# Gate and up values of layer 1 by seven block products in place of eight

## The chip, the cores and the metric

The kernel runs on one core of one Trainium2 chip. The metric is the device time of one execution in microseconds (us): the median of three runs before the change is 770.57 us (769.84 to 771.42). The core has a matrix engine (TensorE, PE in the profile; its weight loads are PEld), a vector engine (VectorE, DVE), an activation engine (ScalarE, ACT), a general engine (GpSimd, POOL) and a queue for transfers (SyncE, SP). All data are float32 but the small flags of the sparsifying, which are bfloat16.

## The reference

Two layers work on `x` of shape 4 x 512 x 256. Each is a layer norm, an attention part and an MLP part on the same normed rows, added to `x`. Layer 0 is an mLSTM with an MLP, and a mixture of low-rank experts. The change touches layer 1 alone:

```python
xn = _layernorm(x, axis=-1)
x = x + _L1_attn_ref(xn, L1_attn_weight_qkv, L1_attn_weight_out) \
      + _L1_ffn_ref(xn, L1_ffn_w_gate, L1_ffn_w_up, L1_ffn_w_down)

# attention: l is the batch of 4, n the 512 positions: each position attends over the 4 rows
attn = jnp.einsum('lnhd,mnhd->nhlm', q, k)            # 16 heads of 16
causal = jnp.tril(jnp.ones((l, l), dtype=bool))
attn = jax.nn.softmax(jnp.where(causal, attn, -jnp.inf), axis=-1)
out = jnp.einsum('nhlm,mnhd->lnhd', attn, v).reshape(l, n, e)
return jnp.einsum('lne,fe->lnf', out, weight_out)

# MLP: 256 -> 1024 -> 256; of each four neighbours of h the two largest stay
h = jax.nn.silu(x @ w_gate) * (x @ w_up)
return _sparsify_2to4(h) @ w_down
```

The attention is causal over the four rows of the batch, so the first row attends to itself alone, with weight one, whatever its q.

## The kernel before

A *block* is 128 positions of all four batch rows, 512 columns once transposed; there are four blocks. Partitions hold features or positions, 128 at a time.

Layer 1's rows are normed (`layernorm`), transposed on PE into `xnT` (2 tiles of 128 features x 512 columns; `front_rows`), and then used by three streams. `rows(j)` goes over the 1024 inner features in tiles of 128, in two groups of four: for each tile two matrix products (`project`, one for each 128 of the 256 input features) make `gp` from the gate weights and ACT takes its Silu; two more make `up`, and DVE multiplies them into `hs`. The weights' columns are laid out so that the four tiles of a group hold the four neighbours of the 2:4 rule, which `sparsified` then applies with DVE comparisons on `hm`, the absolute values. `attention_rows(j)` makes q, k and v for each of the four batch rows and `attend_rows` the scores, with products on POOL (`pd`) and sums on DVE (`sc`, `st`, `o`). `finish_rows(j)` sums attention (`oT` with `aoT`) and MLP (`hs` with `f_down`) in PSUM (`yp`), adds them to `x` on DVE and stores.

The order is made when the program is built. The streams are Python generators; `Flow` asks each when it could go on, by a clock of estimated ends (`Clock`), and takes the next that is ready; ties go by `turn`. `flow.wait` yields the time at which named tiles, and so many of the eight PSUM banks, will be there; `flow.soon` asks again a little later. What comes out is one fixed order for each engine (`keep_in_program_order`), which each engine follows strictly. At run time only semaphores are waited for, so an instruction that waits holds all behind it on its engine.

SBUF is reused across layers by tag: layer 1's gate weights lie where layer 0's `wguT` was, its up weights in `lora`, its q, k, v weights in `WdT`, its down weights in `w_gate`. The profile names tiles by these tags: `gp<-xnT,wguT` is layer 1's gate, `up<-xnT,lora` its up, `yp<-w_gate,hs` its down. All recorded instructions carry the line of one helper (L221), so groups are told apart by their tiles.

Of the kernel before, what the change touches and what calls it, by code (L numbers as in the profile page):

```python
# [9 lines left out]
AF = mybir.ActivationFunctionType  # L10
# [17 lines left out]
FAR = 3.0e4  # L28
BANKS = 8
AHEAD = 4  # L30


@with_exitstack
def layers_kernel(ctx: ExitStack, tc: tile.TileContext, io: dict, out: bass.AP):
# [193 lines left out]
    class Flow:  # L228
# [29 lines left out]
        def spare(self):  # L258

            return max(clock.free["dve"], self.now + 0.2)  # L260

        def wait(self, *aps, banks=0, over=False):

            while True:
                t = clock.ready(*aps, reads=over)
                room = clock.room(banks) if banks else 0.0
                if room > 1e8:
                    room = self.soon()
                yield max(t, room)
                if not banks or clock.room(banks) <= self.now:  # L270
                    return
# [201 lines left out]
    def project(ps, w, xT, lo, n):  # L473

        for k in range(KD):
            mm(ps[0:n, :], w[:, k, lo : lo + n], xT[:, k, :], start=(k == 0), stop=(k == KD - 1))

# [902 lines left out]


    qkvT = weight("qkvT", 3 * D, "WdT", NFC * D)
    f_gate = weight("f_gate", FF, "wguT", 4 * DFF)
    f_up = weight("f_up", FF, "lora", 2 * DFF + NFC * E * R)
    f_down = weight("f_down", D, "w_gate")
    aoT = weight("aoT", D, "w_out")


    with ExitStack() as l1:
# [3 lines left out]

        def attend_rows(j, q, k, v):

            sc = new(sm, [P, B, B, AH], "sc", 2)
            pool.memset(sc, LOWEST)
            for l in range(B):  # L1400
                m = l + 1
                pd = new(wk1, [P, B, D], "pd", 2)
                pool.tensor_tensor(
                    out=pd[:, 0:m, :], in0=k[:, 0:m, :],
                    in1=q[:, l : l + 1, :].to_broadcast([P, m, D]), op=ALU.mult)
                yield from flow.wait(pd)
                dve.tensor_reduce(
                    sc[:, l, 0:m, :], pd[:, 0:m, :].rearrange("p m (h d) -> p m h d", d=ADH),
                    AX.X, ALU.add)
            st = new(sm, [P, B, AH], "st", 2)  # L1410
            by_m = sc.rearrange("p l m h -> p l h m")
            dve.tensor_reduce(st, by_m, AX.X, ALU.max)
            stb = st.unsqueeze(2).to_broadcast([P, B, B, AH])
            dve.tensor_tensor(sc, sc, stb, ALU.subtract)
            act.activation(sc, sc, AF.Exp)
            yield from flow.wait(sc)
            dve.tensor_reduce(st, by_m, AX.X, ALU.add)
            dve.reciprocal(st, st)
            dve.tensor_tensor(sc, sc, stb, ALU.mult)
            o = new(wk1, [P, B, D], "o", 1)  # L1420
            for l in range(B):
                m = l + 1
                pd = new(wk1, [P, B, D], "pd", 2)
                pool.tensor_tensor(
                    out=pd[:, 0:m, :].rearrange("p m (h d) -> p (m h) d", d=ADH),
                    in0=v[:, 0:m, :].rearrange("p m (h d) -> p (m h) d", d=ADH),
                    in1=sc[:, l, 0:m, :].rearrange("p m h -> p (m h)").unsqueeze(2).to_broadcast(
                        [P, m * AH, ADH]),
                    op=ALU.mult)
                yield from flow.wait(pd)  # L1430
                dve.tensor_reduce(
                    o[:, l, :], pd[:, 0:m, :].rearrange("p m c -> p c m"), AX.X, ALU.add)
            while j >= 2 and j - 2 not in out_of:
                yield flow.soon()
            oT = new(wk1, [P, KD, S], "oT", 2)
            for k in range(KD):
                yield from flow.wait(o, banks=1)
                transposed(lambda l, k: o[:, l, k * P : (k + 1) * P], oT, k)
            outs[j] = oT

        def sparsified(j, hs):


            BF = mybir.dt.bfloat16

            def flags(n, tag, bufs=2):
                return new(wk1, [P, n, S], tag, bufs, BF)

            hm = new(wk1, [P, 4, S], "hm", 2)
            for n in range(0, 4, 2):  # L1450
                yield from flow.wait(hs[:, n : n + 2, :])
                act.activation(hm[:, n : n + 2, :], hs[:, n : n + 2, :], AF.Abs)
            yield from flow.wait(hm)

            c0123 = flags(2, "c0123")
            dve.tensor_tensor(c0123, hm[:, 0:4:2, :], hm[:, 1:4:2, :], ALU.is_ge)
            yield flow.soon()
            c0213 = flags(2, "c0213")
            dve.tensor_tensor(c0213, hm[:, 0:2, :], hm[:, 2:4, :], ALU.is_ge)
            yield flow.soon()  # L1460
            rest = flags(2, "rest", 1)
            c12, d30 = rest[:, 0, :], rest[:, 1, :]
            dve.tensor_tensor(c12, hm[:, 1, :], hm[:, 2, :], ALU.is_ge)
            dve.tensor_tensor(d30, hm[:, 3, :], hm[:, 0, :], ALU.is_gt)
            yield flow.soon()

            t03, t21 = flags(2, "t03", 1), flags(2, "t21", 1)
            dve.tensor_tensor(t03, c0123, c0213, ALU.add)
            dve.tensor_tensor(
                t21, c0213, rest[:, 0:1, :].to_broadcast([P, 2, S]), ALU.add)  # L1470
            yield flow.soon()
            keep = new(wk1, [P, 4, S], "keep", 2, BF)
            for n, (t, other, op) in enumerate((
                    (t03[:, 0, :], d30, ALU.is_gt), (t21[:, 1, :], c0123[:, 0, :], ALU.is_gt),
                    (t21[:, 0, :], c0123[:, 1, :], ALU.is_le), (t03[:, 1, :], d30, ALU.is_le))):
                dve.tensor_tensor(keep[:, n, :], t, other, op)
            yield flow.soon()
            for n in range(0, 4, 2):
                dve.tensor_tensor(
                    hs[:, n : n + 2, :], keep[:, n : n + 2, :], hs[:, n : n + 2, :], ALU.mult)  # L1480
                yield flow.soon()
            halves.setdefault(j, []).append(hs)

        def finish_rows(j):
# [40 lines left out]
        def attention_rows(j):  # L1525
            while j not in xTs:
                yield flow.soon()
            xT = xTs[j]
            q, k, v = (new(wk1, [P, B, D], n, 1) for n in "qkv")
            for l in range(B):  # L1530
                for name, lo, n in (("qk_ps", 0, 2 * D), ("v_ps", 2 * D, D)):
                    yield from flow.wait(xT, banks=1)
                    ps = mm_ps(name)
                    for kk in range(KD):
                        mm(ps[:, 0:n], xT[:, kk, l * P : (l + 1) * P], qkvT[:, kk, lo : lo + n],
                           start=(kk == 0), stop=(kk == KD - 1))
                    if lo == 0:
                        act.mul(q[:, l, :], ps[:, 0:D], ADH**-0.5)
                        act.copy(k[:, l, :], ps[:, D : 2 * D])
                    else:  # L1540
                        act.copy(v[:, l, :], ps[:, 0:D])
            yield from attend_rows(j, q, k, v)

        def attention_of_all_rows():
            for j in range(NJ):
                yield from attention_rows(j)

        def rows(j):
            xT = xTs[j]
            if j + 1 < NJ:  # L1550
                flow.add(front_rows(j + 1), 10)
            for f0 in range(0, NF, 4):
                hs = new(wk1, [P, 4, S], "hs", 4)
                gated.setdefault(j, []).append(hs)
                for n in range(4):
                    yield from flow.wait(banks=1)
                    gp = mm_ps("gp")
                    project(gp, f_gate, xT, (f0 + n) * P, P)
                    act.activation(hs[:, n, :], gp, AF.Silu)
                    yield from flow.wait(banks=1)  # L1560
                    up = mm_ps("up")
                    project(up, f_up, xT, (f0 + n) * P, P)
                    dve.tensor_tensor(hs[:, n, :], up, hs[:, n, :], ALU.mult)
                flow.add(sparsified(j, hs))
            flow.add(finish_rows(j), turn=1)

        def all_rows():
            for j in range(NJ):
                flow.until(lambda: j in xTs)
                yield from rows(j)  # L1570
            written.add(NJ - 1)

        flow.add(attention_of_all_rows())
        flow.run(all_rows())
        flow.until(lambda: not flow.streams)


# [38 lines left out]
```

## Time and profile before

| | us |
|---|---|
| median of three runs | 770.57 (769.84 to 771.42) |
| the profiled execution's own time | 770.89 |
| its span, first to last instruction | 769.1 |
| around the span | 1.8 |
| layer 1, from the first `qk_ps` on PE to the end | 230.1 |
| PE busy / weight loads | 762.4 / 518.2 |
| DVE / ACT / POOL busy | 466.9 / 225.1 / 162.8 |

A row of a group gives the operation, the tiles (out from in), the shapes and the count, then busy time, the mean of one in ns, and the idle time of its engine just before, with what ended it. PE's rows include the time in which a product runs through the pipeline, beside the next one; the chain of work shows the spacing. The clock that was granted to PE was 1.0 in all slices.

### The profile page before, as it was taken

How to read it: one execution, taken by the hardware profiler on the slowest of the kernel's cores; microseconds unless marked ns; L12 is line 12 of the kernel's file. 1: busy time of each engine (PE TensorE's matmuls, PEld its weight loads, DVE VectorE, ACT ScalarE, POOL GpSimd, SP SyncE). 2: the span in 40 equal slices, each digit the busy share in tenths (PEclk: the TensorE clock that was granted, in tenths of full speed). 3: DMA queues.
4: the chain of work that ended last, by engine and by line, in shares of the span. 5: the costliest groups of instructions: out<-in, count | busy, mean ns of one | idle time of the engine just before them, and what ended most of it. 6: DMA issues, size and time to landing. Idle time of an engine off the chain costs nothing.

```text
span 769.1 us, 9739 instructions
## 1 busy us (share of the span) xinstructions
PE 762.4 (99%) x3792; PEld 518.2 (67%) x3792; DVE 466.9 (61%) x1075; ACT 225.1 (29%) x457; POOL 162.8 (21%) x154
## 2 busy tenths in 40 slices
PE   9999999999999999999999999999999999999998
PEld 6786777766667875865777774747545664664487
DVE  6787576956544987633377635341376965934971
ACT  4334224332313343212133312010444224214300
POOL 6221051232041320240030041000333224013100
PEclk9999999999999999999999999999999999999999
DMA  7930000300000200000031110001000000000001
GB/s 236 291 109 1 2 1 0 97 15 0 2 1 1 111 0 1 2 1 0 1 111 36 75 43 13 1 0 55 0 1 0 1 27 1 0 29 0 1 14 42
DMA packets 18959, 25.44 MB, mean 33 GB/s; under 512 B 2784, under 2 KB 12768, under 8 KB 18912
## 3 DMA queue, kind: packets, MB, share of 16 engines
q1 hardware_dynamic: 17824, 24.53, 9.9%
q8 instruction: 30, 0.49, 0.3%
q10 hardware_dynamic: 1088, 0.28, 0.2%
q14 instruction: 17, 0.14, 0.1%
HBM read 22.65 MB, written 2.16 MB: 32 GB/s over the span
## 4 chain that ended last, share of the span: by engine, by line
PE 91%; DVE 8%; issue 1%; DMA 0%; POOL 0%; ACT 0%; SPq 0%; DVEq 0%; POOLq 0%
PE yp L221 18%; PE chunk L221 16%; PE up L221 14%; PE gp L221 14%; PE acc L221 10%; PE qk_ps L221 4%; PE pt L221 2%; PE vp L221 2%; PE o_ps L221 2%; PE v_ps L221 2%; PE lp L221 2%; DVE sl L221 1%; PE qk L221 1%; PE hv L221 1%; DVE tmp L221 1%; PE q_ps L221 1%
## 5 line engine op out<-in xcount | busy, mean ns | idle before, releaser
L221 PE MATMUL chunk<-low,lora 128*128 128x256 f32 (+1 forms) x384 | 86.3, 384 | 1.3 <-DVE he_pair L221 1.1
L221 ACT ACTIVATE sl<-chunk 128x256 f32<-128x256 f32 x132 | 50.7, 384 | 113.7 <-PE chunk L221 100.9
L221 PE MATMUL chunk<-xnT,wguT 128*128 128x256 f32 (+1 forms) x384 | 83.8, 383 | 0.0
L221 PEld LDWEIGHTS chunk<-xnT,wguT 128*128 128x128 f32 (+1 forms) x384 | 63.7, 181 | 20.5 <-issue 8.9
L221 PEld LDWEIGHTS chunk<-low,lora 128*128 128x128 f32 (+1 forms) x384 | 63.5, 181 | 17.1 <-issue 4.4
L221 DVE SCALAR_TENSOR_TENSOR sl<-sl,chunk 128x256 f32<-128x256 f32 x132 | 54.6, 414 | 23.9 <-ACT sl L221 23.5
L221 PE MATMUL up<-featT,w_up 128*128 128x512 f32 x128 | 60.4, 594 | 0.0
L221 PE MATMUL gp<-featT,w_gate 128*128 128x512 f32 x128 | 60.3, 593 | 0.0
L221 PE MATMUL up<-xnT,lora 128*128 128x512 f32 x128 | 60.2, 592 | 0.0
L221 PE MATMUL gp<-xnT,wguT 128*128 128x512 f32 x128 | 60.2, 592 | 0.0
L221 PE MATMUL yp<-w_down,hid 128*128 128x256 f32 x256 | 56.4, 379 | 0.0
L221 PE MATMUL yp<-w_gate,hs 128*128 128x256 f32 x256 | 56.1, 379 | 0.0
L221 PEld LDWEIGHTS yp<-w_down,hid 128*128 128x128 f32 x256 | 48.5, 190 | 8.2 <-issue 1.9
L221 PEld LDWEIGHTS yp<-w_gate,hs 128*128 128x128 f32 x256 | 48.6, 190 | 6.6
L221 DVE SCALAR_TENSOR_TENSOR tmp<-tmp,gp 128x512 f32<-128x512 f32 x32 | 22.0, 687 | 45.6 <-ACT tmp L221 45.6
L221 ACT ACTIVATE tmp<-gp 128x512 f32<-128x512 f32 x32 | 19.1, 597 | 95.0 <-PE gp L221 95.0
L221 POOL TENSOR_TENSOR pd<-k,q 128x256 f32<-128x256 f32 (+3 forms) x16 | 24.6, 1539 | 97.8 <-ACT k L221 96.5
L221 PEld LDWEIGHTS gp<-xnT,wguT 128*128 128x128 f32 x128 | 24.2, 190 | 28.8 <-issue 28.0
L221 PEld LDWEIGHTS up<-xnT,lora 128*128 128x128 f32 x128 | 24.2, 190 | 28.4 <-issue 27.5
L221 PEld LDWEIGHTS gp<-featT,w_gate 128*128 128x128 f32 x128 | 24.2, 190 | 28.1 <-issue 27.7
L221 PEld LDWEIGHTS up<-featT,w_up 128*128 128x128 f32 x128 | 23.9, 190 | 27.2 <-issue 26.1
L221 PE MATMUL acc<-tmp,lora 128*128 128x512 f32 x80 | 40.8, 598 | 0.0
(221 smaller groups left out, 1188.3 us busy)
## 6 DMA issues: line engine op xcount, KB each, us to landing
ct<-m_dram SPq DMA_DIRECT2D x8, 1024.0 KB, 8.5
x<-in_x SPq DMA_DIRECT2D x3, 512.0 KB, 9.7
out<-x SPq DMA_DIRECT2D x6, 256.0 KB, 2.2
w_gate<-in_w_gate SPq DMA_DIRECT2D x1, 1024.0 KB, 7.0
w_up<-in_w_up SPq DMA_DIRECT2D x1, 1024.0 KB, 7.6
w_down<-in_w_down SPq DMA_DIRECT2D x1, 1024.0 KB, 10.2
wguT<-in_f_gate SPq DMA_DIRECT2D x1, 1024.0 KB, 5.0
lora<-in_f_up SPq DMA_DIRECT2D x1, 1024.0 KB, 4.9
```

What stands on the lines that cost most here:

```text
L221: return tc.keep_in_program_order(f(*args, **kw))
```

## The change

Gate and up values of a group of four inner tiles are made from blocks. The weights of two tiles are taken as a 2 x 2 matrix of blocks (`a11` ... `a22`: input half by tile parity), the transposed rows as another (`b11` ... `b22`: input half by column half, 256 columns each). Strassen's scheme, in Winograd's form, replaces eight block products by seven and needs sums of blocks: `sides` makes those of the weights once, on POOL, into room that layer 0 has left; `other_sides` makes those of the rows (`xd`) for each block, on DVE for the first and on POOL for the others. The sums after the products are made in PSUM: `Sevens.pairs` adds products into banks `x`, `y` and `z`, and takes copies of what stands in them at a point, on ACT (into `z`, and into SBUF rooms cut from `w_up` and `w_down`), which DVE adds later. The four quarters of a result reach `gate` or `up` through `took`: Silu on ACT; the multiply on DVE for the first column half and on POOL for the second. One identity product writes bank `z` at the start.

Besides, the first batch row's q and its scores are left out, and its attention output is a copy of v; the layer's streams get other waits and turns (`unhurried`, `turn`, the start of `attend_rows` as a stream of its own), and `all_rows` becomes one of them.

```diff
+        def unhurried(self):
+            while True:
+                yield max(clock.free["dve"] - LITTLE, self.now + 0.1)
+                if clock.free["dve"] <= self.now + LITTLE:
+                    return
...
+    def sides(w, rooms, by):
+        v = w.rearrange("p k (q m c) -> p k q m c", m=2, c=P)
+        for i in range(len(rooms) // 3):
+            q = slice(2 * i, 2 * i + 2)
+            a11, a12, a21, a22 = v[:, 0, q, 0, :], v[:, 1, q, 0, :], v[:, 0, q, 1, :], v[:, 1, q, 1, :]
+            s1, s2, s4 = rooms[3 * i : 3 * i + 3]
+            for o, a, b, op in ((s1, a21, a22, ALU.add), (s2, s1, a11, ALU.subtract),
+                                (a21, a11, a21, ALU.subtract), (s4, a12, s2, ALU.subtract)):
+                by.tensor_tensor(out=o, in0=a, in1=b, op=op)
...
+    def other_sides(xT, t, by):
+        b11, b12, b21, b22 = (xT[:, k, h * HALF : (h + 1) * HALF] for k in range(2) for h in range(2))
+        for n, a, b in ((0, b12, b11), (1, b22, t[:, 0, :]), (2, b22, b12), (3, b21, t[:, 1, :])):
+            by.tensor_tensor(out=t[:, n, :], in0=a, in1=b, op=ALU.subtract)
...
+            def product(ps, m, n, start=False, stop=False):
+                for i in range(2):
+                    mm(ps[:, i * HALF : (i + 1) * HALF], a[m](q0 + i), b[n],
+                       start=start and i == 0, stop=stop and i == 1, skip_group_check=True)
...
+            def added(ps, t, m, half):
...
+                    yield from flow.wait(ps, t)
+                    dve.tensor_tensor(t, ps, t, ALU.add)
...
+                    took(m, half, t, lambda: None)
+                flow.add(rest(), turn=-2)
...
+            def first():
+                yield from flow.wait(*b.values(), banks=2)
+                x, y = (mm_ps(n) for n in "xy")
...
+                product(x, "a11", "b11", start=True)
+                while self.users:
+                    yield flow.soon(0.2)
+                self.users += 1
+                act.copy(z, x)
+                yield 0
+                product(y, "s1", "t1", start=True)
+                t2 = copied(y)
+                yield from read(x)
+                product(x, "s2", "t2")
+                t3 = copied(x)
+                yield clock.ready(z)
+                product(z, "a12", "b21", stop=True)
+                took(0, 0, z, free_z)
+                yield from read(y)
+                product(y, "s4", "b22", stop=True)
+                added(y, t3, 0, 1)
+                kept.extend((x, t2))
+            def last():
+                x, t = kept
+                yield from read(x)
+                product(x, "s3", "t3")
+                added(x, t, 1, 1)
+                yield from read(x)
+                product(x, "a22", "t4", stop=True)
+                took(1, 0, x, lambda: clock.held.discard(x.tensor.name))
...
+    gate_sides, up_sides = (sides(w, rooms[i : i + 6], pool) for w, i in ((f_gate, 0), (f_up, 6)))
...
-            for l in range(B):
+            for l in range(1, B):
...
+            act.copy(o[:, 0, :], v[:, 0, :])
...
-                for name, lo, n in (("qk_ps", 0, 2 * D), ("v_ps", 2 * D, D)):
+                for name, lo, n in (("qk_ps", 0 if l else D, 2 * D if l else D), ("v_ps", 2 * D, D)):
...
+        sevens = Sevens(room)
+        mm(sevens.z, ident, xTs[0][:, 0, :], start=True, stop=True)
...
+        def following_rows(j):
+            yield from front_rows(j)
+            bs[j] = other_sides(xTs[j], room_of_sides(), pool)
...
-                for n in range(4):
-                    yield from flow.wait(banks=1)
-                    gp = mm_ps("gp")
-                    project(gp, f_gate, xT, (f0 + n) * P, P)
-                    act.activation(hs[:, n, :], gp, AF.Silu)
-                    yield from flow.wait(banks=1)
-                    up = mm_ps("up")
-                    project(up, f_up, xT, (f0 + n) * P, P)
-                    dve.tensor_tensor(hs[:, n, :], up, hs[:, n, :], ALU.mult)
-                flow.add(sparsified(j, hs))
...
+                        u = t.rearrange("p (i n) -> p i n", i=2)
+                        if half:
+                            pool.tensor_tensor(out=h, in0=u, in1=h, op=ALU.mult)
+                        else:
+                            dve.tensor_tensor(h, u, h, ALU.mult)
...
+                for a, took in ((gate_sides, gate), (up_sides, up)):
+                    first, last = sevens.pairs(a, b, f0 // 2, took)
+                    yield from first
+                    flow.add(last)
+                flow.add(then(), turn=-1)
             flow.add(finish_rows(j), turn=1)
...
-        flow.add(attention_of_all_rows())
-        flow.run(all_rows())
+        flow.add(all_rows())
+        flow.add(attention_of_all_rows())
         flow.until(lambda: not flow.streams)
```

## The prediction

> **What bounds the kernel now.** I read the busy shares first, then layer 1 alone as one stretch, then the chain that ended last, then groups by shape, and for single hand-offs the timeline. The names are those of the diff: a call of `pairs` makes products P1 to P7 in its order (P1 `a11·b11`, P2 `s1·t1`, P3 `s2·t2`, P4 `a12·b21`, P5 `s4·b22`, P6 `s3·t3`, P7 `a22·t4`). A, B, C, D before a number are a block's four calls in order: gate and up of the first four tiles, gate and up of the last four.
>
> Busy shares, then the stretch from 539 us (layer 1's first `qk_ps`) to the end; its columns are the stretch's length, then PE, PEld, DVE, ACT, POOL busy us with counts, and the granted clock:
> ```profile
> PE 762.4 (99%) x3792; PEld 518.2 (67%) x3792; DVE 466.9 (61%) x1075; ACT 225.1 (29%) x457; POOL 162.8 (21%) x154
> ...
> 539.00:769.10 230.10, 226.90 (x762) 139.49 (x760) 145.61 (x230) 71.01 (x123) 50.70 (x38) 1.00 0.03 10
> ```
> TensorE (PE) is the bound in every part, at full clock, and in layer 1 it is idle only at the very end. So what a change takes off PE shows in the time, if no wait replaces it.
>
> The chain in order of time (start, us, what), two places in layer 1:
> ```profile
> 559.96 1.72 PE gp L221 x4
> 561.67 1.72 PE up L221 x4
> ...
> 731.45 34.55 PE yp L221 x160
> 766.00 0.02 issue
> 766.02 0.42 DVE x L221
> ```
> Four 512-wide instructions take 1.72 us, 0.4295 each; 160 of 256 columns take 34.55 us, 0.2159 each. A float32 product is two instructions.
>
> Groups by shape (busy, mean ns of one | idle before):
> ```profile
> L221 PE MATMUL gp<-xnT,wguT 128*128 128x512 f32 x128 | 60.2, 592 | 0.0
> L221 PE MATMUL yp<-w_gate,hs 128*128 128x256 f32 x256 | 56.1, 379 | 0.0
> L221 PEld LDWEIGHTS yp<-w_gate,hs 128*128 128x128 f32 x256 | 48.6, 190 | 6.6
> L221 ACT COPY oT<-pt 128x512 f32<-128x512 f32 x8 | 4.3, 591 | 0.1
> L221 DVE TENSOR_TENSOR hs<-up,hs 128x512 f32<-128x512 f32 x32 | 21.9, 684 | 28.2 <-PE up L221 22.2 <-ACT hs L221 4.8 <-ACT hm L221 1.2
> L221 POOL TENSOR_TENSOR pd<-k,q 128x512 f32<-128x512 f32 x4 | 5.1, 1268 | 7.2 <-ACT k L221 7.2
> ```
> The means of PE (592, 379) hold 0.163 us of pipeline beyond the issue spacing; only the spacing adds up. The weight load of 190 ns lies under each 216 ns instruction.
>
> **The change, part by part.**
>
> *Products.* Before, gate and up of layer 1 are 256 instructions of 512 columns: 256 x 0.4295 = 110.0 us. After, there are 16 calls (4 blocks of rows, 2 groups of four tiles, gate and up) of 7 products of 2 x 2 instructions of 256 columns: 448 x 0.2159 = 96.7 us. PE: -13.2. Unlike gate's, a weight load now comes per 256 columns, as in `yp`, whose spacing I used.
>
> *q of the first row.* One `qk_ps` per block goes from 512 to 256 columns: 4 x 0.86 = -3.4 us of PE. Its ACT, POOL and DVE work goes too: ACT 4 x 0.384, replaced by a copy `o<-v` of 0.37; POOL 4 x (0.73 + 0.62); DVE 4 x (0.42 + 0.41) and a quarter of the score operations, some 5.3 us.
>
> *`z`.* One identity product of 512 columns: +0.86.
>
> PE in sum: -13.2 - 3.4 + 0.9 = **-15.8 us**.
>
> *Weight sides on POOL.* 16 operations of 128x256, 0.73 each by `pd<-k,q 128x256`: 11.7 us. POOL's order puts them behind the `rstd` at 491.2 and the next POOL work of before starts at 541.9. `f_up` was issued at 432.6 and landed 4.9 us later. So they run from 492 to 504 beside layer 0's MLP, and block 0's transposed rows are not needed before 539: nothing. Were that room gone, 11.7 us would stand before P2. No DMA moves: SP's order is the same, and so is every engine's up to layer 1 but for these.
>
> *Sides of the rows* (`xd`): block 0 has four DVE operations (0.42 each) after layer 0's last `x<-yp`, done some 2.6 us into layer 1; P1 starts after 11.2 us of `z`, `qk_ps`, `v_ps` and transposes. The other blocks' 12 operations are POOL's (8.7 us), one block ahead: nothing.
>
> *Copies and adds.* ACT gets three 128x512 copies a call, 48 x 0.59 = 28.3 us; DVE two adds from PSUM, 32 x 0.684 = 21.9, and gives half of the up multiplies (16 x 0.684 = 10.9) to POOL, where they cost 16 x 1.27 = 20.3. Two table loads fewer (9 to 7). Layer 1 in sum, against some 214 us: DVE 145.6 + 21.9 - 10.9 + 1.7 - 5.3 = 153 (71%); ACT 71 + 28.3 - 2.6 = 97; POOL 50.7 + 20.3 + 8.7 - 5.4 = 74. None becomes the bound by its sum.
>
> *New waits on PE.* P3 writes `x` again, so it waits for ACT's copy of P1; P7 waits for DVE's add that reads P6; a call's P1 copy into `z` waits for the last call's reader of `z`. A PE wait holds all products behind it. Where P1, P2, P3 follow each other: P1 issues to 0.864, is readable at 1.03, ACT is done at 1.03 + 0.03 + 0.59 = 1.65, P3 is due at 1.73: no wait, margin 0.08 less the hand-back. ACT never writes PSUM in this trace; its copies from PSUM to SBUF (0.59) are the nearest row, and a 128x1024 one (1.05, `hm`) an upper bound: 0.4 x 16 = +6 us. I take 0.59, the same size and engine. P7: in the built order at least 2.6 us of other products stand between P6 and P7 (C6 to C7 in the last block: D3, D4, D5), against 0.16 + 0.68 + 0.1 = 0.95 for the add, if DVE is free.
>
> DVE is densest in block 1, where the first block's second sparsifying, the next block's layernorm and block 1's attention meet. Walked with these durations from a free DVE, it has no gap for some 15 us; the reader of `z` ends 0.8 us later than the bank is written, which costs `x` of the next P3 0.1 us, and the transposes wait 0.45 us for `xn`. That is 0.6 us in the worst block. There POOL matters:
> ```profile
> 568.89 1.21 DVE L221 TENSOR_TENSOR c<-hm 128x1024 bf16<-128x1024 f32 x1
> 572.16 1.71 DVE L221 TENSOR_TENSOR c<-hm 128x1024 bf16<-128x1024 f32 x1
> ...
> 570.85 1.94 POOL L221 TENSOR_TENSOR pd<-v,sc 128x1024 f32<-128x1024 f32 x1 [3.00 <-DVE o L221]
> ```
> The same comparison takes 1.21 us alone and 1.71 when it starts under a POOL operation, ending 1.1 us after that one's end. 28 more such operations (29 us) could lengthen DVE by nothing to 29 us. [...] Even 153 + 29 = 182 us leaves DVE under PE, so it costs only where PE waits for DVE. Zero waits is the low end; one hold of 1.27 us for each of the 16 P7 less its slack of 1.6 us is still nothing, but queued behind a sparsifying step of 2.4 us it is 2 us a call in blocks 1 and 2, up to +8. I take **+1.5 us**, near the walk.
>
> *The end.* After the last P7, 24.2 us of `yp` (row block 2: 13.8; block 3's attention and first half: 10.4) cover the last sparsifying, which waits on DVE behind `x2<-yp` until 13.8 and then needs some 7.5 us: 21.4. It holds by 2.8 us, so the end stays `yp`, `x`, store, as before.
>
> Sum on the profiled execution: 770.9 - 15.8 + 1.5 = 756.6; the median of the runs is 0.3 below the profiled one: **756.3 us**.
>
> **Rivals.**
>
> (R1) *Hand-offs eat half.* ACT's write to PSUM is slow (+6) or DVE's adds come late in blocks 1 and 2 (+8): about 764. For it: DVE's 71% and the POOL hold above; against it: the slack in the order.
>
> (R2) *Every return waits; slower.* Place: P3 and P7, the two products that write a bank just read. If nothing stood in between, each would cost a read (0.16 + 0.68 + 0.1 = 0.95): 32 x 0.95 = 30, so 785. It decides from 1.0 us of waiting a call (15.8 / 16). Against it: layer 0's `chunk` accumulates in the same way, with ACT and DVE reading between the steps, and in its longest run in the chain 56 of them take 11.64 us, 0.208 each.
>
> (R3) *Weight loads show; slower.* 192 more weight loads of 0.19 us on PE would be +36.5: 791. The `yp` spacing (0.216 with a 0.190 load each) speaks against it: a load that could not overlap would give 0.406. [...]
>
> **How the numbers follow.** Mine 0.72 (its own range 754.5 to 759), R1 0.18, R2 0.05, R3 0.03, and 0.02 for a gain eaten to within the noise. No waits at all gives 754.8; take 0.7 off for rates: low 754. The high end takes in R1: 766. What this kernel's runs can tell from no change is about 0.2%, 1.5 us. Faster: 0.72 + 0.18 = 0.90; within: 0.02; slower: 0.08.
>
> **What would show it.** Right: `qk_ps` starts at 539 as before; `x`, `y`, `z` products sum to 448 instructions at 0.216 us; PE idle in layer 1 under 3 us; ACT's `z<-x` near 0.59; the chain still PE; the last DVE `hs` ends before its `yp`. Wrong: PE idle before `x` released by DVE `w_up` or `w_down` or by ACT (R1 or R2), products above 0.22 us (R3), or a PE wait before the last 16 `yp`.

## The result and the profile after

The median of four runs is **763.99 us** (763.43 to 766.31), against 770.97 (769.84 to 771.42) before on the same chip: a ratio of 0.9918 [0.9906, 0.993]. The change makes the kernel 7.0 us faster by the medians (6.3 by the ratio), where 14.3 were forecast. The direction and the range (754 to 766) hold; the likeliest time, 756.3 with its own range to 759, does not. The time of rival R1 (764) came out, mostly by another way than R1's, as shown below.

The profiled execution of after is the slowest of its four, 766.31 us with a span of 764.6, so it shows a little more loss than the median has. Its busy shares, and the chain's shares by engine, from the page:

```profile
PE 752.8 (98%) x3986; PEld 557.4 (73%) x3986; DVE 493.3 (65%) x1087; ACT 247.4 (32%) x503; POOL 206.3 (27%) x190
...
PE 81%; DVE 17%; issue 1%; ACT 1%; POOL 0%; DMA 0%; DVEq 0%; POOLq 0%
```

Layer 1 as one stretch (length; PE, PEld, DVE, ACT, POOL busy us with counts; granted clock; DMA share; GB/s):

```profile
540.00:770.00 230.00, 216.59 (x955) 177.80 (x953) 169.65 (x242) 93.59 (x169) 83.57 (x59) 0.98 0.03 10
```

DVE has 17% of the chain, where before had 8. The span ends at 764.6, so PE is idle for 8.0 us of 224.6 in layer 1, against 3.2 of 230.0, all at the end, before. DVE is busy there for 169.65 us, where the sum gave 153, and the granted clock is 0.98 instead of 1.00.

Three places of the chain in order of time (start, us, what): the first block's products, the place that lost most, and the end.

```profile
551.45 0.86 PE x L222 x4
552.31 0.86 PE y L222 x4
...
599.80 0.60 DVE w_down L222
600.40 4.15 DVE xn L222 x3
604.55 0.04 issue
604.59 1.65 PE pt L222 x6
606.24 1.71 PE z L222 x4
...
730.37 31.09 PE yp L222 x144
```

A product of four instructions takes 0.86 us, as forecast, and the end is the unbroken run of `yp` that was forecast. But at 600.40 the chain leaves PE: three `xn` take 4.15 us on DVE, and the product behind them takes 1.71 us, twice its 0.86.

What lay under these `xn`, from the timelines of DVE, POOL and PE (start, us, engine and line, operation, out from in; in brackets the idle time before and what ended it):

```profile
600.32 4.54 DVE L222 TENSOR_SCALAR xn<-x,mv,rstd 128x256 f32<-128x256 f32 x4
...
599.68 1.50 POOL L222 TENSOR_TENSOR pd<-v,sc 128x768 f32<-128x768 f32 x1
601.13 1.32 POOL L222 TENSOR_TENSOR hs<-w_down,hs 128x512 f32<-128x512 f32 x1
602.41 1.98 POOL L222 TENSOR_TENSOR pd<-v,sc 128x1024 f32<-128x1024 f32 x1
...
602.65 0.33 PE L222 MATMUL pt<-ident,xn 128*128 128x128 f32 x1 [0.89 <-DVE xn L222]
604.59 1.65 PE L222 MATMUL pt<-ident,xn 128*128 128x128 f32 x6 [1.61 <-DVE xn L222]
```

Three POOL operations follow each other without a gap; the four `xn` start under the first and end just after the last. PE stands before the transposes twice, and all products behind them wait with it.

A smaller wait, at 593, is at a hand-off for which the prediction had slack, P6 to P7 of block 1's first gate call (PE's timeline):

```profile
591.16 1.03 PE L222 MATMUL x<-xd,wguT 128*128 128x256 f32 x4
592.02 1.03 PE L222 MATMUL x<-xd,lora 128*128 128x256 f32 x4
594.00 1.10 PE L222 MATMUL x<-xd,wguT 128*128 128x256 f32 x4 [0.95 <-DVE w_up L222]
```

The first row is P6 and the last P7; between them stands one other product, 0.86 us.

The granted clock about that place (columns as in the stretch above):

```profile
600.00:605.00 5.00, 2.50 (x11) 1.34 (x10) 5.00 (x6) 1.63 (x3) 4.39 (x3) 0.89 0.00 0
605.00:611.00 6.00, 6.00 (x19) 4.99 (x19) 6.00 (x6) 1.77 (x3) 5.32 (x5) 0.52 0.00 0
611.00:620.00 9.00, 9.00 (x46) 7.82 (x45) 6.96 (x14) 4.61 (x10) 0.78 (x2) 1.00 0.00 1
```

PE is busy for half of the first five microseconds. Then it has work without a break, but six microseconds at 0.52 of its clock; after that the full clock is back.

To sum up what PE lost, take the distance from the start of each PE instruction of layer 1 to the start of the next, less the issue spacing of its size (0.4295, 0.2159 and 0.1088 us for 512, 256 and 128 columns). What is left is called *slip* below. After has 10.6 us of it: 7.5 of waits (2.9 before the `xn` transposes at 601 to 605, 1.4 before a P7 at 593, 1.25 before transposes at 636, 1.2 before those of `o` at 653, the rest small) and 3.1 of half clock behind the first of these. The forecast had +1.5 for it. A further 0.8 us of the profiled execution lies ahead of layer 1, whose first product starts at 540.00 instead of 539.17; in the profiled executions of the other kernels below it starts between 538.4 and 540.3. So 9.1 more slip and 0.8 of late start make 9.9, against the 9.7 by which the profiled execution missed its sum (766.3 against 756.6).

The groups of DVE and POOL that hold the difference (busy, mean ns of one | idle before):

```profile
L222 DVE TENSOR_TENSOR c<-hm 128x1024 bf16<-128x1024 f32 x16 | 23.3, 1480 | 4.6 <-ACT hm L222 4.6
L222 DVE TENSOR_TENSOR hs<-keep,hs 128x1024 f32<-128x1024 bf16 x16 | 22.1, 1402 | 0.0
...
L222 DVE TENSOR_SCALAR xn<-x,mv,rstd 128x256 f32<-128x256 f32 x12 | 11.9, 1049 | 1.1 <-POOL rstd L222 1.1
L222 DVE TENSOR_TENSOR w_up<-x,w_up 128x512 f32<-128x512 f32 x16 | 11.0, 685 | 9.5 <-PE x L222 9.5
...
L222 POOL TENSOR_TENSOR hs<-w_down,hs 128x512 f32<-128x512 f32 x8 | 15.2, 1894 | 52.6 <-DVE w_down L222 52.6
```

The first three of them in before:

```profile
L221 DVE TENSOR_TENSOR c<-hm 128x1024 bf16<-128x1024 f32 x16 | 20.9, 1318 | 0.0
L221 DVE TENSOR_TENSOR hs<-keep,hs 128x1024 f32<-128x1024 bf16 x16 | 19.3, 1214 | 0.0
...
L221 DVE TENSOR_SCALAR xn<-x,mv,rstd 128x256 f32<-128x256 f32 x12 | 6.1, 567 | 1.1 <-POOL rstd L221 1.1
```

Their means were 1318, 1214 and 567 ns. The adds from PSUM (`w_up<-x`) stay at their 685. POOL's multiply was priced at 1268 and takes 1894 in these eight, 1534 in the eight from `w_up`. That it is held as well is inferred from this; no run isolates it.

### The profile page after: what moved, and what is told of

Same layout as the page of the kernel before. It is cut to its first block, busy times and chain, and to the rows that moved or that the text cites. A ratio compares the mean times of both kernels' runs of the same rounds, so it can differ in the third digit from the quotient of the medians.

```text
span 764.6 us, 10254 instructions
## 1 busy us (share of the span) xinstructions
PE 752.8 (98%) x3986; PEld 557.4 (73%) x3986; DVE 493.3 (65%) x1087; ACT 247.4 (32%) x503; POOL 206.3 (27%) x190
## 4 chain that ended last, share of the span: by engine, by line
PE 81%; DVE 17%; issue 1%; ACT 1%; POOL 0%; DMA 0%; DVEq 0%; POOLq 0%
PE yp L222 16%; PE chunk L222 14%; PE acc L222 9%; PE up L222 7%; PE gp L222 7%; PE x L222 6%; PE y L222 3%; PE qk_ps L222 2%; PE pt L222 2%; DVE xn L222 2%; DVE sl L222 2%; PE vp L222 2%; PE o_ps L222 2%; PE lp L222 2%; PE z L222 2%; DVE tmp L222 2%
## 5 line engine op out<-in xcount | busy, mean ns | idle before, releaser
L222 POOL TENSOR_TENSOR ss<-ss,mhalf 128x32 f32<-128x32 f32 x4 | 22.1, 5526 | 73.1 <-DVE ss L222 73.1
L222 PE MATMUL acc<-WdT,hid 128*128 128x256 f32 (+1 forms) x192 | 40.6, 384 | 0.0
L222 PEld LDWEIGHTS acc<-WdT,hid 128*128 128x128 f32 (+1 forms) x192 | 32.9, 189 | 6.6 <-issue 2.3
L222 POOL TENSOR_TENSOR rstd<-rstd,mhalf 128x4 f32<-128x4 f32 (+1 forms) x11 | 9.6, 872 | 101.4 <-DVE rstd L222 68.7
L222 DVE TENSOR_TENSOR tmp<-chunk,sl 128x256 f32<-128x256 f32 x80 | 33.9, 424 | 2.8
```

The lines of the kernel that those rows point to most:

```text
L222: return tc.keep_in_program_order(f(*args, **kw))
```

## The experiments

The theory after the result: POOL's operations that read SBUF hold up DVE's operations there (T1, *holds*), DVE is then late for PE, and where PE stands as it does at 601 to 605 (2.5 us of 3.1) the half clock comes on top. Its rivals: the sums of work or the order alone make DVE late, whatever POOL reads (T2, *order*); or the new products themselves, or the rest of the change, cost more than priced (T3). Each kernel ran four times or more, beside the kernel before on the same chip; diffs are against after where nothing else is said. A re-planned kernel is one whose planner found another order.

### Which part of the change misses its price

**The new streams without first-row q, eight products.** Gate and up are made as before, so products, sides, copies and adds of the scheme fall away; the rest of the change stays.

```diff
-        sevens = Sevens(room)
-        mm(sevens.z, ident, xTs[0][:, 0, :], start=True, stop=True)
...
+                for n in range(4):
+                    yield from flow.wait(banks=1)
+                    gp = mm_ps("gp")
+                    project(gp, f_gate, xTs[j], (f0 + n) * P, P)
+                    act.activation(hs[:, n, :], gp, AF.Silu)
+                    yield from flow.wait(banks=1)
+                    up = mm_ps("up")
+                    project(up, f_up, xTs[j], (f0 + n) * P, P)
+                    dve.tensor_tensor(hs[:, n, :], up, hs[:, n, :], ALU.mult)
...
-                for a, took in ((gate_sides, gate), (up_sides, up)):
-                    first, last = sevens.pairs(a, b, f0 // 2, took)
```

> The changed kernel's new streams, turns and waits and its missing first q, but gate and up from eight products as before, no sides, no z. PE has 3.4 us less than before. If the streams cost nothing by themselves: 767 to 768.5. If the new order brings waits of its own: 769 to 772.

Measured: 766.61 (766.49 to 768.11), ratio 0.9948 [0.9931, 0.9965] to a before of 771.28, with 0.1 us of slip and not one wait of PE in layer 1. That is a little faster than both expected ranges. So 4.7 us come from the streams and the left-out q (priced at 3.4, inside the interval of 2.7 to 5.3); in the profiled executions layer 1 is 3.6 us shorter than in before. The seven products bring only the 2.6 us from here to 763.99, where 12.3 (13.2 less 0.86) were priced. The miss is in what the products bring with them.

**Before, with only the first row's q left out.**

```diff
-            for l in range(B):
+            for l in range(1, B):
...
+            act.copy(o[:, 0, :], v[:, 0, :])
...
-                for name, lo, n in (("qk_ps", 0, 2 * D), ("v_ps", 2 * D, D)):
+                for name, lo, n in (("qk_ps", 0 if l else D, 2 * D if l else D), ("v_ps", 2 * D, D)):
```

(against before)

> The kernel before with the first row's q and scores left out and nothing else of the change. By the price of the prediction PE loses 4 x 0.86 = 3.4 us and nothing comes in its place: 767.5, 0.9955 of before. A rival, that the shorter attention moves a wait, gives 768.5 to 771.

Measured: 769.65 (768.65 to 769.87, ten runs), ratio 0.9981 [0.9972, 0.999]: 1.4 us, not 3.4. PE's waits in layer 1 (total us, times, longest) say why:

```profile
PE pt L221 <- DVE o L221: 1.1, 1, 1.1
```

Before had no such wait. With less PE work before them, the transposes of `o` at 574 us come ahead of DVE's sums, and slip rises from 0.2 to 2.0 us, this wait the most of it. So the rival expectation, that a wait moves, came out. In the new streams there is no such wait.

### Holds or order

**POOL multiplies shortened.** Same order on every engine; the 16 multiplies of up values on POOL touch one of 256 columns.

```diff
-                            pool.tensor_tensor(out=h, in0=u, in1=h, op=ALU.mult)
+                            clock.issue("pool", "tensor_tensor", (),
+                                        dict(out=h, in0=u, in1=h, op=ALU.mult))
+                            tc.keep_in_program_order(nc.gpsimd.tensor_tensor(
+                                out=h[:, :, 0:1], in0=u[:, :, 0:1], in1=h[:, :, 0:1],
+                                op=ALU.mult))
```

> The changed kernel with every engine's order kept; the 16 POOL multiplies of the up values do one column of 256 in each row of tiles and leave the rest of the product out. Hold theory (POOL's reads of SBUF hold DVE's two-input and layernorm instructions, so PE's transposes and P7 wait): DVE's lengthening against the means of before, some 17 us, falls below 9, PE's waits in layer 1 fall from 7.5 to some 3 us, the four xn of block 1 take under 3 us instead of 4.5, and the time is 758 to 760.5. Rival (DVE simply has too much work of its own with the 32 adds): DVE's own work and order are the same, the waits stay near 7 us, 763 to 765.

Measured: 762.19 (761.17 to 763.25), ratio 0.9891 [0.9875, 0.9908]. DVE in layer 1 falls from 169.65 to 164.52, though nothing of its own work is gone, and slip from 10.6 to 6.3. The wait for `xn` shrinks to 1.7 us and does not vanish, because `pd` still lies there. The result is between what the two theories gave: the multiplies hold DVE, but they are a part of it only.

**Up multiplies on DVE.** POOL loses its 16 multiplies, DVE gets them; re-planned.

```diff
-                        if half:
-                            pool.tensor_tensor(out=h, in0=u, in1=h, op=ALU.mult)
-                        else:
-                            dve.tensor_tensor(h, u, h, ALU.mult)
+                        dve.tensor_tensor(h, u, h, ALU.mult)
```

> All up multiplies on DVE, as before the change, the order planned anew. DVE gets 16 x 0.684 = 10.9 us of work of its own, POOL loses 27.5 us. Hold theory: the holds that go are worth at least as much as the added work, 759 to 763. Rival (too much work on DVE): later by some of the 10.9 us, 766 to 770.

Measured: 767.93 (767.71 to 768.27), ratio 0.9962 [0.9947, 0.9976], slower than after. The time is in the rival's range, and the number of the holds theory missed. DVE's sum is 168.17, hardly less: 10.9 us of new work take the place of the holds. PE's longest wait in layer 1:

```profile
PE pt L222 <- ACT sc L222: 5.7, 1, 5.7
```

The view puts it down to ACT's `sc`, which runs from 628.53 to 628.90; what the transposes read is `xn`, whose first operation ends at about the same time.

The DVE and POOL operations behind it, from their timelines:

```profile
622.89 1.79 DVE L222 TENSOR_SCALAR rstd<-mv 128x4 f32<-128x4 f32 x1
...
622.31 2.35 POOL L222 TENSOR_TENSOR pd<-k,q 128x1024 f32<-128x1024 f32 x1 [0.32 <-ACT k L222]
...
628.42 1.38 DVE L222 TENSOR_SCALAR xn<-x,mv,rstd 128x256 f32<-128x256 f32 x4
```

The stretch after it, columns as above:

```profile
629.00:635.00 6.00, 6.00 (x18) 4.83 (x19) 4.98 (x12) 4.37 (x7) 2.46 (x2) 0.50 0.01 3
```

The new order puts the last block's transposes where its `rstd` has to pass from DVE to POOL and back. A DVE operation on four elements, `rstd<-mv` (0.16 us in before), takes 1.79 us, ending when `pd` ends; POOL's power follows at 624.76, and when it is done DVE is in the middle of other work, so that `xn` starts at 628.42. One 5.7 us wait, and six more microseconds at half clock: 13.2 us of slip. So a hold of some 1.6 us stands at the start of this wait, and 2.65 more are DVE's own work in that order. The same four `xn` take 1.38 us here, with POOL idle, against 4.54 in after.

**`xn` on ACT.** From the second block on, the normed rows are made by ACT; re-planned. In after, ACT's operations on SBUF took no longer beside POOL's reading ones: two `hm` in a row 2.02 us under `pd` at 573, 2.00 beside an idle POOL at 731.

```diff
+            dve.scalar_tensor_tensor(off, mv[:, :, 0], -1.0, rstd, ALU.mult, ALU.mult)
+            for b in range(B):
+                act.activation(xn[:, b, :], x[:, b, :], AF.Identity, bias=off[:, b : b + 1],
+                               scale=rstd[:, b : b + 1])
+            return
```

> The changed kernel with the last step of layer 1's layernorm (12 xn, 11.9 us of DVE, up to 1.7 us each) on ACT, some 0.55 us each, the order planned anew. Hold theory: ACT shares nothing with POOL, the transposes' waits of 3.0 + 1.3 us go, and the clock's drop behind them: 758.5 to 761. Rival (DVE full of its own work): DVE loses only 4 us of own work, waits move to P7: 762 to 764.

Measured: 762.37 (761.64 to 763.18), ratio 0.9889 [0.9875, 0.9904]. DVE falls to 159.5, the clock is 1.000 in every run, and no wait for `xn` is left. Others have come:

```profile
PE x L222 <- ACT z L222: 3.7, 4, 1.7
PE pt L222 <- DVE o L222: 1.9, 1, 1.9
```

The slip is still 7.2 us. The longest of these waits, 1.7 us at 602, is for a copy into `z` that stands in ACT's queue behind three `xn` (from 597.69) and four other operations. The waits for `xn` and the half clock went, as the holds theory said, but the time is in the rival's range, and other waits came, as the rival said, though at P3 and the transposes of `o` and not at P7.

**POOL writes instead of reads.** Same order on every engine, same time on POOL. Each operation of layer 1 on POOL with two tensors becomes one on a few columns and two fills of its whole output; the differences and products themselves are left out.

```diff
+    def written(name, **kw):
+        clock.issue("pool", name, (), kw)
...
+        fs = [lambda: nc.gpsimd.tensor_tensor(
+            out=few(kw["out"]), in0=few(kw["in0"]), in1=few(kw["in1"]), op=kw["op"])]
+        fs += 2 * [lambda: nc.gpsimd.memset(kw["out"], 0.5)]
...
-                pool.tensor_tensor(
+                written(
+                    "tensor_tensor",
                     out=pd[:, 0:m, :], in0=k[:, 0:m, :],
...
-                            pool.tensor_tensor(out=h, in0=u, in1=h, op=ALU.mult)
+                            written("tensor_tensor", out=h, in0=u, in1=h, op=ALU.mult)
```

> The changed kernel with every engine's order kept; each two-input POOL operation of layer 1 (pd, xd, the up multiplies) is replaced by the same operation on one column, which still waits for its inputs, and two fills of its whole output, so that POOL takes about as long but hardly reads SBUF; the products themselves are left out. Hold theory: DVE's instructions take what they take alone (c 1.21, four xn 1.4 us together), the waits of PE in layer 1 fall from 7.5 to under 2.5 us, 757 to 760. Rival (DVE's own work, and POOL's lateness, not its reads): waits stay over 5 us, 761.5 to 764.

Measured: **756.48** (755.95 to 757.26), ratio 0.9811 [0.9797, 0.9826]. Layer 1 as one stretch:

```profile
540.00:770.00 230.00, 210.79 (x951) 175.13 (x950) 150.11 (x240) 93.43 (x169) 84.06 (x163) 1.00 0.03 10
```

The only wait of PE listed in it is one of 0.3 us for `xn`. The four `xn` that took 4.54 us in after:

```profile
597.39 2.36 DVE L222 TENSOR_SCALAR xn<-x,mv,rstd 128x256 f32<-128x256 f32 x4
```

They start 58.6 us after layer 1's first product, against 60.3 in after. So of the 3.9 us by which they end earlier, 2.2 lie under the `xn` themselves and 1.7 are lateness that DVE had before. The DVE groups held most in after:

```profile
L222 DVE TENSOR_TENSOR c<-hm 128x1024 bf16<-128x1024 f32 x16 | 19.3, 1226 | 4.6 <-ACT hm L222 4.6
L222 DVE TENSOR_TENSOR hs<-keep,hs 128x1024 f32<-128x1024 bf16 x16 | 19.1, 1216 | 0.0
...
L222 DVE TENSOR_SCALAR xn<-x,mv,rstd 128x256 f32<-128x256 f32 x12 | 6.7, 616 | 1.1 <-POOL rstd L222 1.1
```

POOL is as busy (84.06 against 83.57), in the same order, and DVE does the same operations; they take 150.1 instead of 169.7 us. The slip is 1.5 us, the clock 1.0 in every run; the time is even 0.5 us below the range that the holds theory gave. This separates the theories: the order and the sums alone cost next to nothing, and POOL's reading, with the half clock that its waits bring, costs 7.5 us of the time. The shares of `pd`, `xd` and the multiplies were not told apart beyond the 1.8 us of the shortened multiplies.

### The half clock

**PE kept busy in the long wait.** The kernel with the up multiplies on DVE, with 24 identity products (48 instructions) before the last block's transposes, where it waited 5.7 us. They add nothing to the output.

```diff
+        for _ in range(busy):
+            tc.keep_in_program_order(
+                nc.tensor.matmul(pt[:, 0:P], ident, ident, start=True, stop=True))
...
+            transposed(lambda l, k: xn[:, l, k * P : (k + 1) * P], xT, k,
+                       busy=24 if j == 3 and k == 0 else 0)
```

> e2_up_on_dve with 24 identity products of 128 columns (0.22 us each, 5.2 us) written into the bank of the last block's transposes just before these, where PE waited 5.9 us and then ran about 6 us at half clock. If the idle time brings the half clock: no half clock there, 764.5 to 766 against 767.9. If not: the same 767.5 to 768.5.

Measured: 769.53 (769.02 to 770.66, ten runs), ratio 0.998 [0.9971, 0.999]: not faster than the 767.93 without them, and the expected total missed. The local effect is there all the same. The 16 `yp` behind the transposes, first without and then with the identity products (timelines of the two kernels):

```profile
630.97 5.67 PE L222 MATMUL yp<-w_out,oT 128*128 128x256 f32 x16
```

```profile
623.04 5.52 PE L476 MATMUL pt<-ident 128*128 128x128 f32 x48
628.83 1.73 PE L222 MATMUL pt<-ident,xn 128*128 128x128 f32 x8 [0.26 <-DVE xn L222]
630.40 3.62 PE L222 MATMUL yp<-w_out,oT 128*128 128x256 f32 x16
...
654.43 1.82 PE L222 MATMUL v_ps<-WdT,xnT 128*128 128x256 f32 x4 [3.13 <-DVE x L222]
```

With PE busy the clock does not fall, 1.00 is granted from 623 to 635 instead of 0.94 and then 0.50: 16 `yp` take 3.62 us instead of 5.67. But the won 2.6 us end at 651 before `v_ps`, which waits for DVE's `x<-yp` to give a bank back. That add starts at 653.69 here and at 653.74 without the products: DVE is what counts up to there. PE, being earlier, waits 3.1 us instead of 0.6, and falls to half clock behind this wait too (the four instructions of `v_ps` take 1.82 us instead of 1.13; 0.87 is granted from 651 to 656). This is the whole of the loss: both kernels start that `v_ps` 115.7 us after layer 1's first product, and in the eight microseconds behind it the slip is 1.8 us with the identity products and 0.1 without, which makes the 1.6 us between the two spans (767.6 and 766.0).

### What a better order gets back

Five kernels move PE's instructions away from DVE's late results; none leaves anything out.

**The planner counts the full hold.** Its model of DVE had the hold at no more than an operation's own length; in layer 1 it now lasts to the end of POOL's work.

```diff
-                us += max(0.0, min(us, self.free["pool"] - start))
+                held = max(0.0, self.free["pool"] - start)
+                us += held if self.layer else min(us, held)
```

> The changed kernel; in layer 1 the planner counts a DVE instruction with two SBUF inputs, or a tensor_scalar, as held until POOL's issued work ends, where it counted at most the instruction's own length. Same instructions, another order. Hold theory: the order puts other products where the changed kernel waits for xn and o, waits fall to 3 to 5 us, 759 to 762. Rival: nothing else is ready there, or the estimate of POOL is no better, 763 to 766.

Measured: 761.64 (761.0 to 762.78), ratio 0.9879 [0.9864, 0.9894], 7.0 us of slip. The time is in the range that the holds theory gave, though the waits, 5.4 of the slip, are above its 3 to 5. The `xn` wait stays (2.5 us); the half clock behind it is shorter (1.5 us of slip instead of 3.1; 0.53 granted from 604 to 607).

**Margins.** The transposes of `xn` are let come 4.0 us after the planner's estimate of it, those of `o` 2.5 and P7 1.2, so that other products go ahead.

```diff
+                yield flow.soon(1.2)
+                yield from read(x)
                 product(x, "a22", "t4", stop=True)
...
+        if j:
+            yield from flow.wait(xn)
+            yield flow.soon(4.0)
...
+            yield from flow.wait(o)
+            yield flow.soon(2.5)
```

> The changed kernel with margins in layer 1's plan: the transposes of xn come no sooner than 4 us after their planned readiness, those of the attention output 2.5 us, P7 1.2 us; the planner puts other work before them. Nothing is taken from DVE or POOL. If PE's waits are a matter of place (other products are ready while DVE is held): waits fall from 7.5 to 2 to 4 us, 758 to 761. If DVE, held, is what the later parts wait for anyway, the waits come elsewhere: 762 to 765.

Measured: 762.0 (760.8 to 763.54), ratio 0.9884 [0.9866, 0.9902], 6.7 us of slip. The waits for `xn` and P7 are gone (0.5 left), one for `o` has 2.3 us, and ACT's copies bring three new ones of 0.5 to 0.9. The time is at the edge of the range for waits that come elsewhere, not in the one for a matter of place.

**Both together.** The edits of the last two kernels.

> The margins together with the planner's full count of holds. Place theory: 757.5 to 760.5. Else, as without margins, 761 to 763.

Measured: 760.43 (760.04 to 760.84), ratio 0.9862 [0.9847, 0.9877], 6.1 us of slip, clock 1.000 in every run. This is in the range of the place theory, at its upper end.

**Margins and `xn` on ACT.** The margin before the transposes is 2.0 here, since the `xn` are ACT's.

```diff
-        yield from layernorm(both, x_sb[j], xn)
+        yield from layernorm(both, x_sb[j], xn, by_act=j > 0)
...
+            yield flow.soon(2.0)
```

> The margins (2 us for xn) with the layernorm's last step on ACT, which takes 12 held instructions, some 10 us, off DVE. Place theory with less to hold: 757 to 760. If ACT's bursts make the copies into z late instead (3.7 us of PE's waits without margins): 761 to 763.

Measured: 760.36 (759.72 to 761.45), ratio 0.9866 [0.985, 0.9882], DVE 159.8, 5.6 us of slip, clock 1.000; 0.4 above the range of the place theory and 0.6 below the other. PE's waits:

```profile
PE pt L222 <- DVE o L222: 1.5, 1, 1.5
PE y L222 <- DVE w_down L222: 1.0, 1, 1.0
PE x L222 <- POOL pd L222: 0.9, 1, 0.9
```

**Margins and up multiplies on DVE.**

> The margins with all up multiplies on DVE, where one wait of 5.9 us for xn and the half clock behind it cost most. Place theory: that wait goes, 759 to 763. If DVE with 10.9 us more of its own work is the limit: 766 to 769.

Measured: 763.99 (763.72 to 764.26), ratio 0.9908 [0.9894, 0.9923]: the 5.7 us wait is gone and with it 3.9 us, but DVE has 171.8 us of work, and a P7 waits 3.0 us for its adds, a P3 1.7 for ACT's copy. The time lies between the two expected ranges, next to that of the place theory.

Four of these five beat both kernels; the fifth, with the up multiplies on DVE, equals after. The best two, margins with the planner's full hold and margins with `xn` on ACT, come to 10.9 us below before instead of 7.0. The waits get shorter and move on to the next late result; the best of these orders still has 4 us more slip than the kernel whose POOL doesn't read.

## Why the prediction was wrong

*Products, -13.2 us.* Right: 0.8636 us a product of four instructions, start to start, wherever nothing waits or throttles. With POOL's reads taken away the kernel runs in 756.5 us, and the "no waits at all" of the prediction, 754.8, plus its slip of 1.5 gives 756.3. So all prices on PE hold together, and the forecast of 756.3 is the time of a kernel whose DVE isn't held.

*q, -3.4.* Agrees in the new streams, where the kernel with eight products has a layer 1 shorter by 3.6 us; alone in the old ones it is worth 1.4.

*Weight sides on POOL, nothing.* Right: 16 operations of 0.72 to 0.77 us ran in layer 0, and no wait of PE goes back to them.

*Copies and adds.* ACT's write to PSUM, for which only the copy to SBUF stood as a row, took 575 ns; 590 was taken, and the upper bound of 1.05 (+6 us) is refuted. The sums of ACT (97, measured 94) and of DVE's own work (153, measured 150 where POOL doesn't read) were right. Not right were the sums under holds: DVE 169.7, inside the bounds of 153 to 182 but far from their lower end, and POOL 84 instead of 74, mostly since its 16 multiplies took 27.5 us instead of 20.3.

***New waits on PE, "I take +1.5 us, near the walk".*** This is the step that failed: 7.5 us of waits in the profiled execution. The walk went "from a free DVE" with unheld durations, and found 0.45 us of waiting before the transposes. The pair of rows that shows the hold stood right behind it, and the value was taken at the wrong end of the bounds from it. That the upper one (+8) is within half a microsecond of the 7.5 is luck: it stood for waits of P7, and P7 waits 1.4; the transposes of `xn` wait some 4.1 and those of `o` 1.2. Nor does the slack hold that was given to P7, "at least 2.6 us of other products": that is C6 to C7 of the last block, while the order has 0.86 us behind the P6 of 591.16 and 1.73 behind others, such as that of 712.94, against the 0.95 that a free DVE needs. What the walk missed is that holds add up in a row: POOL had three reading operations end to end, DVE's four `xn` stood under all of them, and 1.4 us of work became 4.5. DVE's share of the layer, 71% forecast and 76% measured, says nothing on that; the margin of each hand-off under the operations that run at that moment does.

Two groups show which of DVE's operations were lengthened: adds with one input in PSUM kept their 685 ns in after, where `c`, with both in SBUF, took 1480, and under fills `c` fell to 1226.

*The granted clock.* This term was missing from the sum altogether: 3.1 us in the profiled execution. It was priced as if a wait on PE cost its own length.

*The end.* Right: `yp` runs without a break from 730.37 to the last `x`.

*The rivals.* R1 (0.18) came true in its time, mostly by luck. Of its two mechanisms ACT's write is no part of the loss, and late adds of DVE made 1.4 us of waits, not 8. The POOL hold that it named in its favour is the cause, but it cost most at the transposes of `xn` and `o`, and the half clock on top is no part of R1. R2 fell: of 32 hand-offs at P3 and P7, one cost more than 0.3 us in the profiled execution. R3 fell with the spacing.

## What to carry to other kernels

Where the bound engine's waits depend on an engine whose operations a neighbour lengthens (here four `xn` from 1.38 to 4.54 us), walk the order with the long durations, operation by operation, and look above all for several of the neighbour's operations in a row; a busy share with room to spare doesn't price it. Count a wait on TensorE as longer than it is where the granted clock falls behind it: in these traces the half clock behind five waits of 2.5 to 5.7 us (some of them in two parts) cost a further 1.5 to 3.2 us. And when a change puts work onto an engine that lengthens the operations of the one that hands over, moving PE's dependent work later in the order (here 10.9 us gained instead of 7.0) is worth as much as choosing the engine.

## What was not expected of the hardware

**Which DVE operations are held.** A `tensor_scalar` on one SBUF tensor with two per-partition scalars is held too, which the kernel's planner already counted (from more than 64 elements) and the prediction's walk did not: four of `xn` took 1.38 us beside an idle POOL, 4.54 under reading operations, and 2.36 under fills, where an operation with two tensors was free (`c` 1226 ns, against 1.21 us alone in before). Even one of 4 elements a partition, 0.16 us in before, took 1.79 us until POOL's product ended. And POOL's multiplies of 1268 ns took 1894 and 1534 in after's two groups.

**The half clock.** The granted clock fell where PE had stood for 2.5 of 3.1 us (after: 0.50 in each microsecond from 604 to 610), for 5.7 (up multiplies on DVE: 0.50 from 629 to 635), 3.1 (with identity products: 0.87 from 651 to 656), 3.0 (margins and up on DVE: 0.61 from 616 to 619, 0.82 from 619 to 622) and 2.5 in two waits (the planner's full hold: 0.53 from 604 to 607). In the profiled executions with pauses of 1.7 and 1.9 (`xn` on ACT, 540 to 770) and of 2.3 (margins alone, 648 to 658) as the longest it stayed at 1.00. The four runs of after have mean clocks of 0.995, 0.997, 0.998 and 1.000 for 766.3, 763.8, 764.2 and 763.4 us with the same program, so it seems that a pause of this length doesn't always bring it; of the other three no trace shows the pauses. How long a pause has to be is not shown by these runs.
